# Expert layer of a perceiver block: token rows laid out in DRAM by expert, one weight row per expert and partition, six pairs held, eight experts fixed, fourteen narrow

## The chip, the core and the metric

The kernel runs on one core of a Trainium2 chip. A core has a matrix engine (TensorE, PE in the profile; PEld is its weight load), a vector engine (VectorE, DVE), an activation engine (ScalarE, ACT), GpSimd (POOL) and SyncE (SP), and 16 DMA engines that move data between DRAM and on-chip memory. Plain transfers are started by SyncE and ScalarE; transfers whose rows are given by a list of indices (indirect transfers) are started by GpSimd. Each engine works through its own queue in order: an instruction that waits holds up everything behind it in that queue. The metric is the time of one execution on the device, in microseconds.

## The reference

One layer for 256 tokens of width 512: cross-attention to 4096 context tokens, a Mamba-2 mixer, and a mixture of 32 experts with 6 per token beside a shared expert, each with a layer norm ahead and a residual. What the change touches is the last part:

```python
x = x + xattn(layernorm(x), ctx, ...)            # 16 query heads, 4 key heads, 128 wide
x = x + mamba(layernorm(x), ...)                 # inner width 1024
h = layernorm(x)                                 # (256, 512)
scores = sigmoid(h @ gate_w)                     # (256, 32)
topk_w, topk_i = top_k(scores, 6)
topk_w = topk_w / (sum(topk_w) + 1e-20)
combine = sum(one_hot(topk_i, 32) * topk_w[..., None], axis=1)
g = einsum('td,edf->tef', h, wg)                 # wg, wu: (32, 512, 192)
u = einsum('td,edf->tef', h, wu)
routed = einsum('tef,efd,te->td', silu(g) * u, wd, combine)   # wd: (32, 192, 512)
shared = (silu(h @ sg) * (h @ su)) @ sd          # inner width 384
x = x + routed + shared
```

## The kernel before

Tokens are handled as two tiles of 128 (t = 0, 1). Attention takes about the first 750 us, the mixer runs until about 835 us, the experts fill the rest. All matmuls are in 32-bit floats.

**Order of the work.** The program text gives each instruction a priority. A planner replays the program with its own estimates of durations and puts, on each engine, the ready instruction that is earliest in the program first. The order per engine is then fixed; instructions further down in the text may stand earlier in a queue when they are ready earlier. While attention runs, seven large writes of zeros fill the DRAM buffer `xg` (`clear`, L519), so that unused rows are zero.

**Routing.** `route(t)` (L995) turns the normed rows, multiplies them with the gate, takes the best six and builds `hot` (one-hot, 6 x 32) and `mask` (their sum). `ranks(t)` (L1024) gives each token its rank within each expert, by a matmul with a triangular matrix. `places()` (L1033) needs the counts of both tiles. Experts 0 to 9 have fixed places. The other 22 are sorted by their number of tokens: the 10 busiest get places with 128 rows ("wide"), the last 12 get 64 rows each ("narrow"). A place is a position in the order of work. `rows()` (L1072) turns rank and place into a row number for each token and choice; `scatter(t)` (L1017) then writes the token's normed row to each of its six rows of `xg`, with one indirect transfer per choice. `weight_rows()` (L1087) works out from `places` which rows of the weights the gathers read, and writes them to `place`. Experts with more than 64 tokens in a narrow place (or more than 128 anywhere) set `crowded`, and a second, slower pass over all experts follows; the same list of rows sends their surplus tokens to a second region of `xg`, `MAIN` and beyond.

**Rounds.** Experts are worked in 16 pairs. In round n (L1490): gate and up of pair n (`gate_up`, L1394, whose matmuls have the line of the helper L216; narrow: `gate_up_halves`, matmuls L1353), fetch of the rows of pair n+2 (`fetch`, L1326), turning the rows of pair n+1 by TensorE (`turn`, transposes L1338), down of pair n-1 (`down`, L1430 and L1433; narrow: `down_halves`, L1375 and L1376), turning the hidden values of pair n (L1412, narrow L1366). `fetch` is a plain transfer on SyncE, as the rows of a place are at a fixed address. Four buffers hold fetched blocks: a wide pair takes two, a narrow one takes one. Pairs 0 and 1 (experts 0 to 3) are not fetched: TensorE picks their rows with one-hot matrices (`picks`, `ps_pick`, L1447). Results go to the buffer `ye`; the last three pairs are added up in PSUM instead. At the end, 12 indirect gathers (L1294) bring each token's rows back from `ye`, and L1302 adds them with their weights.

**Weights.** A pair has three pieces of 768 KB: gate and up of its first expert, gate and up of its second, and both down matrices. 15 pieces are held at a time (five pairs), in memory that attention and the mixer no longer need. Pieces of pairs 0 to 4 are loaded by SyncE (`load_weights`, L1149 to L1153) when their memory comes free. Later ones are gathered by GpSimd with `gather_weights` (L1158), five indirect transfers a pair: the two gate-up pieces as soon as the piece's previous user has done its gate and up, the down piece after its down.

The scatter and the fetch, as they are:

```python
G.indirect_dma_start(out=xg_rows[t * TOPK + k], in_=xn[:, t, :], in_offset=None,
                     out_offset=bass.IndirectOffsetOnAxis(ap=row[:, t, k:k + 1], axis=0))
...
nc.sync.dma_start(self.rows[n, i], xg[r:r + P, :])
```

Of the kernel before, what the change touches and what calls it, by code (L numbers as in the profile page):

```python
# [19 lines left out]
P = 128  # L20
# [34 lines left out]
NHELD = 5  # L55
FIXED = 2 * NHELD
# [3 lines left out]
TAIL = 6  # L60
ZROW = WIDE * P + (NE - WIDE - TAIL) * HALFP
MAIN = ZROW + TAIL * HALFP

# [8 lines left out]
def perceiver_layer(ctx: ExitStack, tc: tile.TileContext, a: dict, out: bass.AP):  # L72
# [50 lines left out]
    xg = tc.dram_tile((MAIN + NE * L, DM), FP, name="xg")  # L123
# [14 lines left out]
    def layer(ctx, bounded):  # L138
# [16 lines left out]
        place = keep.tile([P, NE - FIXED + (NE - FIXED) // 2], U32, name="place")  # L155
# [363 lines left out]
        def clear(n):  # L519

            blocks = (MAIN + NE * L) // P
            per = -(-blocks // (NC - 1))
            e0, e1 = n * per, min((n + 1) * per, blocks)
            zeros(xg[e0 * P:e1 * P, :].rearrange("(e p) d -> p e d", p=P),
                  xn[:, 0:1, :].to_broadcast([P, e1 - e0, DM]))
            if n == 0:
                for y, r0 in ((ye, ZROW), (ye2, NE * L)):
                    zeros(y[r0:, :], xn[:, 0, :])
# [452 lines left out]
        def routing_memory():  # L981
            r = carve(lacc[:, 1], (P,), (P,), (NE,), (NT, NE), (NT, NE), (NT, NE), (NT, NE), (NT, NE), (NT, 8), (NT, 8),
                      (NT, TOPK), (NT, TOPK), (NT,), (NT * TOPK, NE), (FT, L), (1,), (1,), (1,), (1,), (NE,), (NE,), (NE,), (NE,))
            names = ("iota", "before", "first", "gate", "ev", "mask", "rank", "dst", "m8", "idx", "rowf", "w8", "den", "hot", "act",
                     "p", "free", "key", "pos", "keys", "at", "less", "over")
# [47 lines left out]
        def places():  # L1033


            mask, first, pos, key, keys, at, less, over = (m[n] for n in ("mask", "first", "pos", "key", "keys", "at", "less", "over"))
# [31 lines left out]

            V.tensor_scalar(over, m["iota"][:, 0:NE], float(L), float(MAIN), ALU.mult, ALU.add)
            V.tensor_tensor(over, over, first, ALU.subtract)  # L1070

        def rows():  # L1072
# [4 lines left out]
            V.tensor_scalar(dst, dst, float(P), None, ALU.is_ge)  # L1077
            V.tensor_tensor(dst, dst, by_tile(m["over"]), ALU.mult)
            V.tensor_tensor(dst, dst, rank, ALU.add)
            V.tensor_tensor(dst, dst, by_tile(m["first"]), ALU.add)  # L1080
            for t in range(NT):
                hot = m["hot"][:, t]
                V.tensor_tensor(hot, hot, dst[:, t].unsqueeze(1).to_broadcast([P, TOPK, NE]), ALU.mult)
                V.tensor_reduce(m["rowf"][:, t, :], hot, AX.X, ALU.add)
                V.tensor_copy(row[:, t, :], m["rowf"][:, t, :])

        def weight_rows():  # L1087


            n = NE - FIXED  # L1090
            V.tensor_scalar(place_f[:, 0:n], expert, float(P), m["p"], ALU.mult, ALU.add)
            e2 = expert.rearrange("p (n i) -> p i n", i=2)
            for i in range(2):
                half = slice(i * HALFP, (i + 1) * HALFP)
                V.tensor_scalar(place_f[half, n:], e2[half, i], float(REST), m["p"][half], ALU.mult, ALU.add)
            V.tensor_scalar(place_f[HALFP:, n:], place_f[HALFP:, n:], -float(REST), None, ALU.add)
# [47 lines left out]
        slots, slots_of = [], {}  # L1144

        def load_weights(slot, n, j):

            if j < 2:
                nc.sync.dma_start(slot, a["gu"][2 * n + j])  # L1149
            else:  # L1150
                d = slot.rearrange("p (j n) -> p j n", j=3)
                nc.sync.dma_start(d[:, 0:2], a["down"][2 * n:2 * n + 2].rearrange("e p n -> p e n"))
                nc.sync.dma_start(d[:, 2], a["down_rest"][2 * n:2 * n + 2].rearrange("e p n -> (e p) n"))  # L1153

        def gather_weights(slot, n, j):

            def rows(out, src, c):
                G.indirect_dma_start(out=out, out_offset=None, in_=src.rearrange("e p n -> (e p) n"),  # L1158
                                     in_offset=bass.IndirectOffsetOnAxis(ap=place[:, c:c + 1], axis=0))
            s = 2 * n - FIXED  # L1160
            if j < 2:
                rows(slot, a["gu"], s + j)
            else:
                for i in range(2):
                    rows(slot[:, i * DM:(i + 1) * DM], a["down"], s + i)
                rows(slot[:, 2 * DM:], a["down_rest"], NE - FIXED + s // 2)

        def load_piece(p):
            if p < 3 * NP:
                slots_of[p] = slots[p % (3 * NHELD)]  # L1170
                (load_weights if p < 3 * NHELD else gather_weights)(slots_of[p], p // 3, p % 3)

        def load_into(*tiles):
            for tl in tiles:
                slots.append(carve(tl, (WGU,))[0])
                load_piece(len(slots) - 1)
# [25 lines left out]
        for fs in plan:  # L1202
# [19 lines left out]
        load_into(kv[NC][1])  # L1222
# [11 lines left out]
        load_into(*w_x, lacc[:, 0])  # L1234
# [13 lines left out]
        load_into(*w_z)  # L1248
        route(0)
        assemble(1)  # L1250
        turn_y(1)
        ranks(0)
        product, turn = shared_hidden(0)
        mamba_out(1)
        product()
        load_into(wvc, wkc, ctx0)
        load_into(*w_out)
        n = NE - FIXED
        pick, number, expert, place_f, member, member2, members = carve(
            m["kv", 1], (NT * HEAD, P), (P,), (n,), (n + n // 2,), (TAIL, NE), (TAIL, NE), (4 * TAIL,))  # L1260
# [3 lines left out]
        turn()  # L1264
        route(1)
        shared_down(0)
        product, turn = shared_hidden(1)
        product()
        ranks(1)
        places()  # L1270
        rows()
# [351 lines left out]
```

## Time and profile before

| | |
|---|---|
| median of 3 runs | 1005.68 us (1003.59 to 1006.84) |
| profiled execution | 1007.29 us, span 1005.60 us |
| TensorE busy | 975.4 us, 97% of the span |
| VectorE, ScalarE, GpSimd busy | 498.0, 387.3, 206.8 us |
| moved by the DMA engines | 133.24 MB, 133 GB/s over the span |
| indirect transfers on GpSimd's queue (q0) | 34.35 MB in 8,016 packets |
| stretch of the experts' rounds | from about 848 us to 998 us |

The page divides the span into 40 slices with a digit for the busy share of each engine, and lists groups of instructions by source line. More to the point here are views of a stretch of time: busy times in windows, the chain of work that ended last in order of time (each piece with its start, its length, its engine and its line), the waits of an engine's queue (who waited for whom, us in total, times, longest), and the transfers with their median time from issue to landing. "issue" is time in which an engine waited for nothing that the profile shows.

### The profile page before, as it was taken

The numbers are of one execution on the slowest core, as the hardware profiler recorded it, in microseconds if no ns is written. First come the engines' busy times: TensorE is split into PE (matmuls) and PEld (weight loads), VectorE is DVE, ScalarE is ACT, GpSimd is POOL, SyncE is SP. The second block draws the span as 40 slices with busy tenths as digits, with TensorE's granted clock in tenths as the row PEclk, the third lists the DMA queues.
The fourth block names the chain that finished last, engine by engine and source line by source line (L and its number), as shares of the span: only waits on it lengthen the run. The fifth ranks groups of instructions, "written<-read, shape, count | busy, mean of one in ns | idle before, by whom it ended". The sixth has DMA issues, their size and how long they took to land.

```text
span 1005.6 us, 8991 instructions
## 1 busy us (share of the span) xinstructions
PE 975.4 (97%) x2749; PEld 461.7 (46%) x2749; DVE 498.0 (50%) x992; ACT 387.3 (39%) x853; POOL 206.8 (21%) x214
## 2 busy tenths in 40 slices
PE   7999999999999999999999999999999998799996
PEld 3444444444444444444444444444556554455542
DVE  4455555455454454544544544566796557122124
ACT  3645544443443443443434434442363631122210
POOL 4443002001101100201200200000023313455533
PEclk9999999999999999999999999999999999799999
DMA  9735043123313314305305205410153545899954
GB/s 324 220 72 166 4 128 119 37 74 109 79 31 147 83 22 156 85 6 172 83 1 178 54 10 167 131 38 0 27 201 128 202 137 205 300 351 362 365 202 122
DMA packets 139467, 133.24 MB, mean 133 GB/s; under 512 B 80689, under 2 KB 100050, under 8 KB 138258
## 3 DMA queue, kind: packets, MB, share of 16 engines
q1 hardware_dynamic: 126928, 91.85, 29.3%
q0 software_dynamic: 8016, 34.35, 9.5%
q10 hardware_dynamic: 4466, 6.38, 1.8%
q8 instruction: 24, 0.39, 0.2%
q14 instruction: 33, 0.27, 0.1%
HBM read 89.28 MB, written 43.27 MB: 132 GB/s over the span
## 4 chain that ended last, share of the span: by engine, by line
PE 91%; DMA 3%; DVE 2%; POOL 1%; ACT 1%; issue 1%; SPq 0%; POOLq 0%; DVEq 0%; ACTq 0%
PE oT L590 23%; PE scT L565 23%; PE ps_kv L362 17%; PE ps_egu L216 4%; PE ps_self L216 3%; PE ps_v L216 2%; PE ps_o L786 2%; PE ps_ye L1430 2%; PE ps_k L216 1%; PE ps_xbc L216 1%; PE ps_out L976 1%; PE ps_egu L1353 1%; PE ps_sgu L216 1%; PE xgTp L1338 1%; PE total L1421 1%; DMA xg_sb<-xg 1%
## 5 line engine op out<-in xcount | busy, mean ns | idle before, releaser
L581 DVE TENSOR_TENSOR lacc<-lacc,prT 128x512 f32<-128x512 f32 x256 | 183.1, 716 | 240.3 <-ACT prT L571 239.5
L571 ACT ACTIVATE prT<-scT,bq,rk 128x512 f32<-128x512 f32 x256 | 198.8, 777 | 254.7 <-PE scT L565 242.1
L565 PE MATMUL scT<-qT,kT 128*128 128x512 f32 x536 | 270.9, 593 | 0.0
L590 PE MATMUL oT<-prT,v 128*128 128x512 f32 x528 | 268.1, 593 | 0.9 <-ACT prT L571 0.9
L590 PEld LDWEIGHTS oT<-prT,v 128*128 128x128 f32 x528 | 100.3, 190 | 127.0 <-issue 114.8
L565 PEld LDWEIGHTS scT<-qT,kT 128*128 128x128 f32 x536 | 101.5, 190 | 124.3 <-issue 121.7
L194 POOL TENSOR_TENSOR rk<-pv,mhalf 128x4 f32<-128x4 f32 x32 | 32.3, 1010 | 370.8 <-DVE pv L193 370.8
L362 PE MATMUL ps_kv<-wkv,fast 128*128 128x512 f32 x112 | 53.5, 592 | 0.0
L252 ACT ACTIVATE sq<-kraw 128x128 f32<-128x128 f32 x128 | 35.6, 278 | 45.2 <-DVE kraw L380 43.2
L362 PE MATMUL ps_kv<-wkv,ctx 128*128 128x512 f32 x112 | 52.8, 593 | 0.0
L362 PE MATMUL ps_kv<-fast,fast 128*128 128x512 f32 x112 | 52.6, 593 | 0.0
L596 DVE TENSOR_TENSOR oacc<-oT,oacc 128x512 f32<-128x512 f32 x64 | 43.7, 683 | 0.0
L1405 DVE TENSOR_TENSOR hid<-si,ps_egu 128x128 f32<-128x128 f32 x20 | 5.8, 288 | 62.6 <-ACT si L1403 62.6
L362 PEld LDWEIGHTS ps_kv<-wkv,ctx 128*128 128x128 f32 x112 | 21.3, 190 | 26.7 <-issue 23.6
L362 PEld LDWEIGHTS ps_kv<-wkv,fast 128*128 128x128 f32 x112 | 21.3, 190 | 26.7 <-issue 26.7
L362 PEld LDWEIGHTS ps_kv<-fast,fast 128*128 128x128 f32 x112 | 21.3, 190 | 26.7 <-issue 21.7
L356 POOL TENSOR_TENSOR fast<-ctx 128x512 f32<-128x512 f32 x7 | 9.5, 1363 | 113.1 <-PE ps_kv L362 94.2
L380 DVE TENSOR_TENSOR kraw<-ps_kv,fast 128x256 f32<-128x256 f32 x42 | 17.8, 425 | 28.0 <-PE ps_kv L362 28.0
L786 PE MATMUL ps_o<-wo,qT 128*128 128x512 f32 x64 | 28.8, 593 | 0.0
L216 PE MATMUL ps_self<-wq,xT 128*128 128x512 f32 x64 | 28.1, 593 | 0.0
L601 DVE RECIPROCAL lacc<-ps_l 128x512 f32<-128x512 f32 x8 | 26.8, 3348 | 0.1
L362 PE MATMUL ps_kv<-fast,ctx 128*128 128x512 f32 x56 | 26.3, 593 | 0.0
(379 smaller groups left out, 1127.6 us busy)
## 6 DMA issues: line engine op xcount, KB each, us to landing
xg<-xn SPq DMA_DIRECT2D x6, 3328.0 KB, 11.6
ctx<-in_ctxT_dram SPq DMA_DIRECT2D x7, 1024.0 KB, 5.2
kd<-tr SPq DMA_DIRECT2D x112, 64.0 KB, 2.2
kT<-kd SPq DMA_DIRECT2D x28, 256.0 KB, 2.8
ye<-y_sb ACTq DMA_DIRECT2D x23, 256.0 KB, 6.2
xg_sb<-xg SPq DMA_DIRECT2D x22, 256.0 KB, 7.6
wq<-in_wq_dram SPq DMA_DIRECT2D x4, 1024.0 KB, 14.2
wo<-in_wo_dram SPq DMA_DIRECT2D x4, 1024.0 KB, 8.0
```

The lines of the kernel that those rows point to most:

```text
L194: return G.tensor_tensor(dst, v[:, :n], mhalf[:, :n], ALU.pow)
L216: TE.matmul(ps, lhs(k), rhs_of(k), start=(k == 0), stop=(k == KD - 1))
L252: S.activation(sq[:, h, :], raw[:, h, :], AF.Square, accum_out=ss[:, h:h + 1])
L362: TE.matmul(ps, lhs(k), rhs(k), start=(start and k == 0), stop=(k == 1), skip_group_check=True)
L565: TE.matmul(sc, kT[:, g, i * P:(i + 1) * P], qT[:, t, heads4(g), :].rearrange("p h q -> p (h q)"), start=True, stop=True)
L571: S.activation(pr, sc, AF.Exp, bias=shift, scale=SCALE if r is None else r[:, i, g:g + 1])
L581: V.tensor_tensor(la, la, pr, ALU.add)
L590: TE.matmul(outs[g, t], v[:, i, g * HD:(g + 1) * HD], pr, start=(n == 0), stop=last)
L596: V.tensor_tensor(ov, outs.pop((g, t)), ov, ALU.add)
L601: V.reciprocal(rl, ps)
L786: TE.matmul(m["ps_o", t], aT[:, t, h, :], wo[j][:, h % 4, :], start=(h == 0), stop=(h == NH - 1))
L1430: TE.matmul(ps[i], h[:, i, :], wd[:, i, :], start=True, stop=False)
```

## The change

The rows of `xg` are laid out by expert: the row of a token is 256 times its expert plus its rank (`rows_of`), which needs no place. `rows_of(t)` and `scatter(t)` follow `ranks(t)` for each tile. The old row, now computed by `result_rows` after the picks, is used for the results in `ye` alone. The second region of `xg` goes, so it has 8,192 rows instead of 11,520, and the second pass reads the same rows.

`fetch` of a fixed pair remains a plain transfer on SyncE. That of a later pair becomes an indirect gather on GpSimd, with row numbers that `place_rows` works out from the places: one per block for a wide pair, two half blocks in one gather for a narrow pair.

Eight experts are fixed instead of ten. Then 10 wide places and 14 narrow ones follow (12 before). `experts` in DRAM holds gate, up and the first 128 rows of down of an expert as one row of 2,048 floats per partition. The remaining 64 rows of down of a pair are a piece of their own. A gathered pair takes three indirect transfers. Six pairs are held; four of them are loaded by SyncE, pairs 4 and 5 are gathered as soon as the places are known, and the pair n+5 is loaded after the down product of pair n-1, as a whole. `shared_down(0)` stands ahead of `route(1)`.

```diff
-NHELD = 5
-FIXED = 2 * NHELD
+WEX = WGU + DM
+NHELD = 6
+FIXED = 8
 WIDE = FIXED + 10
...
-    xg = tc.dram_tile((MAIN + NE * L, DM), FP, name="xg")
+    xg = tc.dram_tile((NE * L, DM), FP, name="xg")
...
+        def rows_of(t):
+            V.tensor_scalar(m["dst"][:, t], m["iota"][:, 0:NE], float(L), None, ALU.mult)
+            V.tensor_tensor(m["dst"][:, t], m["dst"][:, t], m["rank"][:, t], ALU.add)
+            V.tensor_tensor(own, m["hot"][:, t], m["dst"][:, t].unsqueeze(1).to_broadcast([P, TOPK, NE]), ALU.mult)
+            V.tensor_reduce(m["rowf"][:, t, :], own, AX.X, ALU.add)
+            V.tensor_copy(row[:, t, :], m["rowf"][:, t, :])
...
+        def place_rows():
+            n, w = NE - FIXED, WIDE - FIXED
+            p, half = m["p"], lambda i: slice(i * HALFP, (i + 1) * HALFP)
+            def pairs(to, experts, per):
+                e2 = experts.rearrange("p (n i) -> p i n", i=2)
+                for i in range(2):
+                    V.tensor_scalar(to[half(i)], e2[half(i), i], float(per), p[half(i)], ALU.mult, ALU.add)
+                V.tensor_scalar(to[half(1)], to[half(1)], -float(HALFP), None, ALU.add)
+            for to, experts, per in ((place_f[:, 0:n], expert, P), (place_f[:, n + n // 2:n + n // 2 + w], expert[:, 0:w], L)):
+                V.tensor_scalar(to, experts, float(per), p, ALU.mult, ALU.add)
+            pairs(place_f[:, n:n + n // 2], expert, REST)
+            pairs(place_f[:, n + n // 2 + w:], expert[:, w:], L)
             V.tensor_copy(place, place_f)
...
+        def rows_at(out, src, c):
+            G.indirect_dma_start(out=out, out_offset=None, in_=src,
+                                 in_offset=bass.IndirectOffsetOnAxis(ap=place[:, c:c + 1], axis=0))
+
+        def load_weights(to, n, fixed):
+            if fixed:
+                for i in range(2):
+                    nc.sync.dma_start(to[i], a["experts"][2 * n + i])
+                nc.sync.dma_start(to[2], a["down_rest"][2 * n:2 * n + 2].rearrange("e p n -> (e p) n"))
             else:
+                s = 2 * n - FIXED
                 for i in range(2):
+                    rows_at(to[i], a["experts"].rearrange("e p n -> (e p) n"), s + i)
+                rows_at(to[2], a["down_rest"].rearrange("e p n -> (e p) n"), NE - FIXED + s // 2)
+
+        def load_pair(n):
+            if n < NP:
+                k = n % NHELD
+                weights[n] = (held[2 * k], held[2 * k + 1], rests[k])
+                load_weights(weights[n], n, 2 * n < FIXED)
...
         ranks(0)
+        rows_of(0)
         product, turn = shared_hidden(0)
         mamba_out(1)
         product()
+        scatter(0)
...
         turn()
+        shared_down(0)
         route(1)
-        shared_down(0)
         product, turn = shared_hidden(1)
         product()
         ranks(1)
+        rows_of(1)
+        scatter(1)
         places()
-        rows()
-        for t in range(NT):
-            scatter(t)
+        place_rows()
...
         shares()
-        weight_rows()
         turn()
         shared_down(1)
+        hold(oacc.rearrange("p t g n -> p (t g n)")[:, 0:WEX], kv[NC][0])
+        for n in range(FIXED // 2, NHELD):
+            load_pair(n)
...
             def fetch(self, n, r0=None):
-                if r0 is None:
-                    r0 = [self.row0(n) + i * P for i in range(self.blocks(n))]
...
+                if r0 is None and 2 * n < FIXED:
+                    r0 = [(2 * n + i) * L for i in range(2)]
+                for i in range(self.blocks(n) if r0 is None else 2):
+                    to = self.rows[n, i] = self.e4.tile([P, DM], FP, tag="xg", name="xg_sb")
+                    if r0 is not None:
+                        nc.sync.dma_start(to, xg[r0[i]:r0[i] + P, :])
+                    else:
+                        first, s = NE - FIXED + (NE - FIXED) // 2, 2 * n - FIXED
+                        rows_at(to, xg, first + (s + i if 2 * n < WIDE else WIDE - FIXED + (2 * n - WIDE) // 2))
...
-                for j in range(2):
-                    load_piece(3 * (n + NHELD) + j)
...
                 if n > 0:
-                    load_piece(3 * (n - 1 + NHELD) + 2)
+                    load_pair(n - 1 + NHELD)
...
-    return {"gu": c(gu.reshape(NE, P, WGU)), "down": c(wd[:, 0:P]), "down_rest": c(wd[:, P:])}
+    return {"experts": c(np.concatenate([gu, wd[:, 0:P]], axis=2)), "down_rest": c(wd[:, P:])}
```

## The prediction

> **What bounds the kernel now.** I read the page first, then the windows of the last 160 us, the chain over 838 to 873, SyncE's waits and the timelines of VectorE, GpSimd and SyncE. TensorE is busy 97% of the span and is itself the chain through attention, so an edit there that leaves its matmuls alone is worth nothing. The windows (columns after the stretch: length, then busy time and instructions of PE, PEld, DVE, ACT and POOL, granted clock, DMA share, GB/s) show the one large hole:
>
> ```profile
> 848.20:862.50 14.30, 14.22 (x45) 7.26 (x43) 4.24 (x20) 2.43 (x7) 10.95 (x12) 1.00 0.57 208
> 862.50:872.70 10.20, 2.87 (x12) 2.50 (x13) 1.32 (x2) 1.12 (x2) 3.93 (x5) 0.61 0.98 364
> 872.70:910.00 37.30, 37.30 (x139) 20.86 (x138) 9.23 (x27) 7.78 (x18) 16.47 (x18) 0.97 0.96 342
> 910.00:945.00 35.00, 35.00 (x133) 19.52 (x133) 6.53 (x20) 8.74 (x20) 17.55 (x19) 1.00 0.99 364
> 945.00:972.00 27.00, 27.00 (x129) 10.62 (x127) 6.32 (x19) 6.63 (x16) 11.34 (x12) 1.00 0.79 294
> ```
>
> Pairs 0 and 1 run until 862.4, then TensorE stands still and its clock falls to 0.61. From 872.7 on it is full, although the transfer engines are 96 to 99% taken. What ends the hole is in the chain (start, length, what) and in SyncE's waits:
>
> ```profile
> 843.46 0.08 DVE row L1085
> ...
> 857.88 2.71 DMA xg<-xn,row
> ...
> 861.25 9.62 DMA xg_sb<-xg
> 870.91 1.12 PE xgTp L1338 x4
> 872.03 0.64 PE hidTp L1412 x3
> 872.67 6.37 PE ps_egu L216 x16
> 879.04 0.87 PE xgTp L1338 x8
> ```
> ```profile
> SPq L1331 <- DMA xg<-xn,row: 19.0, 1, 19.0
> ```
>
> The rows of all twelve scatters are ready only at 843.5, because they need every expert's place. GpSimd then issues twelve scatters, 843.83 to 858.84, one each 1.27 us (0.96 busy, 0.30 issue); the last lands at 860.6. Only then does SyncE fetch pair 2, and the second block lands at 870.87, beside weight gathers GpSimd has just started.
>
> **1. Scatter by expert: the hole goes.** A row is now expert x 256 + rank. Tile 0's six scatters need only its ranks (L1031, 816.74): five small VectorE operations, then 6 x 1.27 = 7.6 us of GpSimd, 818 to 826. Tile 1's ranks are ready at 834.66; its rows at about 835.8, its scatters end at 843.4 and land 2.7 us later (the median of that transfer), 846.1. SyncE has nothing left to wait for: its last fixed load waits for ctx0, free at 811.5. It fetches pairs 2 and 3 (four blocks, 1.05 MB, addresses fixed) at about 846 and shares the engines with the first gathers (pair 4, 2.36 MB): 3.4 MB at 364 GB/s is 9.4 us, landed by 856 even in the worst order. Pair 1's work covers TensorE until 861.29 + 1.13 = 862.42. Without the wait it then needs 0.87 (turn) + 0.48 + 5.16 (gate-up), ending at 868.93 instead of 879.04. **Gain 10.1 us**, the slow clock included (6.37 against 5.16). If the cover failed, each microsecond past 862.4 costs one.
>
> **2. One wide pair turns narrow.** By the chain a wide round is 0.87 + 1.72 + 1.06 + 0.48 + 5.16 = 9.29 us; two narrow gate-ups start at 954.90 and 960.50:
>
> ```profile
> 902.41 5.16 PE ps_egu L216 x16
> 907.58 0.87 PE xgTp L1338 x8
> 908.45 1.72 PE ps_ye L1430 x4
> 910.17 1.06 PE ps_ye L1433 x4
> 911.23 0.48 PE hidTp L1412 x3
> ...
> 954.90 2.73 PE ps_egu L1353 x16
> ...
> 960.50 2.73 PE ps_egu L1353 x16
> ```
>
> One wide fewer, one narrow more: **9.29 - 5.60 = 3.7 us gained**. The narrow experts still fit on these inputs: worked out from the reference's router, the 11th busiest free expert has 43 tokens, 64 fit; the branch for crowded experts is not taken.
>
> **3. VectorE before the first picks: a loss.** The picks start at 841.65, after the x_sb addition (L1139, 840.93), whose bank they need; its matmul was done at 839.57, so VectorE's order sets this. Tile 1's new row operations come before the places: by rows L1107 (0.17), L1108 (0.20), L1471 (0.34), L1473 (0.34), L1085 (0.15), less their overlap, 1.1 us on an engine that is full from 834.5 to 837.3. Behind it, place_rows has four small operations more (0.2 each, as L1095) and three of the old rows (L1076 to L1078, 0.65 together) plus L1070 leave: nothing net. The rest of the old rows and the clamped result rows move behind the picks, beside 7.1 us of pick matmuls, and are wanted only by the gathers at 975. **Take 1.0 us lost**; ends 0 (filling VectorE's 1.2 us idle before L1058) and 2. A gain of up to 2.1, all of TensorE's idle before the picks, stays possible through another order; it sets the low end.
>
> **4. GpSimd in the mixer.** Tile 0's scatters stand around the power at 821.24 (L194), which layernorm and then route(1) wait for. One scatter ahead of it costs at most 1.3 us, and route(1)'s mask is ready at 831.4 while TensorE runs the shared experts until 833.9: hidden. All six ahead: 825.6 - 821.2 = 4.4 us late, about 3.5 of it on TensorE. I take 0, since the power is earlier in the program and ready after two or three scatters; the other end goes into the range.
>
> **5. Weights.** A pair is now three gathers (two of 128 rows of 8 KB, one of 2 KB rows), not five: 3.8 instead of 6.3 us of GpSimd. In all 12 x 3 weight gathers + 17 block fetches = 53 issues against 55. A slot is now given back only after the down product, but with six pairs held a load has five rounds' time. From 843.6, in bytes: 12 pairs x 2.36 + 21 fetches x 0.26 + 22 result blocks x 0.26 = 39.6 MB; at 364 GB/s 109 us, done at 953. Pair 15 is wanted at 982.4 - 12.8 = 969.6, pair 13 at 953.3 with 2 x 2.36 MB (13 us) still behind it. Cost 0; a load late by more than these 13 to 16 us stops TensorE.
>
> **6. Fetches move to GpSimd's queue** from pair 4 on. The rows (issue engine, count, size, median us to landing):
>
> ```profile
> xg_sb<-xg SPq DMA_DIRECT2D x22, 256.0 KB, 7.6
> w_in<-in_down_rest_dram,place POOLq DMA_INDIRECT x5, 8.4
> ```
>
> On SyncE's queue a fetch takes 7.6 us, the last gather of a pair on GpSimd's 8.4: the move costs 0.8 us of latency. A fetch goes out when its buffer is turned (888.80, transposes at 888.17) and is wanted two rounds later (907.41), 18.6 us; narrow ones go four deep (951.78, wanted at 975.4). By the rows nothing. [...] I take 0 and keep 4 for the range. Waits of GpSimd on a buffer hold the loads behind it, but a buffer is turned 2.8 us before the slot of the next load is free.
>
> Smaller zero fill (11,520 to 8,192 rows, hidden behind attention's matmuls; TensorE would wait only if its key blocks came late, and it does not now), wp's memory and the early first load: 0.
>
> **Sum.** -10.1 - 3.7 + 1.0 = -12.8. The profiled execution took 1007.29 us, its span 1005.60: span 992.8, 994.5 in all. It was 1.6 over the median of the runs, so the forecast is 1005.68 - 12.8 = **992.9**. The tail after 972 moves with the rounds: TensorE is busy 25.23 of 25.70 us there, and GpSimd is free well before.
>
> **Rivals.** (a) *As summed*, 992.9, own range 989.5 to 995.5: 0.70. (b) *A new wait ahead of the experts*: six scatters before the power, 3.5 more, 996.4. For it: GpSimd is idle from 818 to 821, so a scatter enters at once; against: the order above. 0.11. (c) *Fetches behind weights*, 4 to 6 more, 997 to 999. For: DMA at 0.99; against: the 18 us lead. 0.12. (d) *The hole stays*: the gathers of pairs 4 and 5 (6 x 1.27) go ahead of tile 1's scatters, the last lands near 860 and pair 2 near 868; only the narrow pair is gained, 1003. Against: rows come before places on VectorE. 0.03. (e) *Slower: transfers pace the rounds*, in the narrow rounds on GpSimd's queue. 39.6 MB must pass; the run ends 3 us later than before when pair 15 lands 15.8 us past its time, at 985, a rate under 39.6 / 142 = 279 GB/s. Rows of 8 KB and gathered blocks are untried; 6 KB and 2 KB rows run at 342 to 364. At 275 the time is 1011. 0.04.
>
> 0.3% is 3 us, about what these runs can tell from no change (they spread over 3.3). Faster 0.70 + 0.11 + 0.12 = 0.93, same 0.03, slower 0.04. The range leaves out (d), (e) and a little of each side: 989.5 to 999.
>
> **What would show it.** Right: scatters in two groups, near 818 and 836; no idle TensorE at 862 and clock 1.00; pair 2's gate-up at 5.16; seven narrow gate-ups instead of six, those after the first 5.60 apart; picks at 842 to 843. Wrong: TensorE waiting on xg_sb or on weights after pair 3, the power (L194) late behind scatters, GB/s under 300 between 870 and 940.

## The result and the profile after

The changed kernel takes **998.55 us** (median of 6 runs, 997.40 to 1000.71) against 1005.73 us of the kernel before (6 runs, 1003.59 to 1006.84): ratio 0.9933, 95% interval 0.9917 to 0.9949, so 7.2 us less. In three later groups of runs the kernel before took 1007.56 to 1008.43 us (medians), and in one of them the changed kernel, run again, 997.79 us (ratio 0.9905, interval 0.989 to 0.992), 10.1 us less. Both kernels spread by 3 to 5 us from run to run. The forecast was 992.9, 12.8 less.

The profiled execution of the changed kernel took 998.33 us with a span of 996.6, 9.0 us below the span before. First the windows of the experts' rounds (columns as before: length, busy time and instructions of PE, PEld, DVE, ACT and POOL, granted clock, DMA share, GB/s):

```profile
846.00:861.25 15.25, 15.25 (x43) 7.62 (x42) 8.67 (x32) 2.31 (x5) 6.96 (x7) 0.94 0.90 350
861.25:866.60 5.35, 5.35 (x17) 2.39 (x15) 0.83 (x4) 0.66 (x2) 1.18 (x2) 1.00 0.46 184
866.60:874.00 7.40, 7.33 (x35) 4.86 (x34) 1.73 (x5) 2.31 (x5) 3.54 (x4) 1.00 0.98 338
874.00:910.00 36.00, 36.00 (x140) 19.92 (x138) 9.14 (x26) 8.52 (x19) 18.91 (x20) 1.00 0.95 343
910.00:945.00 35.00, 35.00 (x146) 17.21 (x145) 7.74 (x23) 8.41 (x19) 16.35 (x18) 1.00 0.99 381
```

TensorE has no hole left: 7.33 of 7.40 us where it had 2.87 of 10.20. The one blemish is the clock of 0.94 at the start. From 866.6 to 945 the transfer engines are as full as before (0.95 to 0.99), and TensorE does not wait for them. The fetch of pairs 2 and 3 goes out at 850.13 (SyncE's timeline, first line here), 3 us after GpSimd's last scatter ends (847.05), where it went out at 860.87 before. The chain of the changed kernel (start, length, what) runs through the place of the hole on TensorE alone:

```profile
850.13 2.18 SPq L1344 DMA_DIRECT2D xg_sb<-xg  x4
```
```profile
844.30 8.83 PE ps_pick L1466 x16
853.13 5.16 PE ps_egu L218 x16
...
866.77 1.02 PE xgTp L1354 x8
867.79 0.33 PE hidTp L1432 x3
...
868.18 5.40 PE ps_egu L218 x16
873.58 0.87 PE xgTp L1354 x8
...
940.14 2.73 PE ps_egu L1373 x16
...
945.74 2.73 PE ps_egu L1373 x16
```

From the start of gate_up(0) (852.97 in TensorE's timeline; 848.62 before) to the end of gate_up(2) it is 20.61 us where it was 30.42. The narrow gate-ups of pairs 10 and 11 start 5.60 apart. There are seven narrow gate-ups, the first at 933.68. But the picks took 8.83 us, where they took 7.13 before:

```profile
841.65 7.13 PE L1447 MATMUL ps_pick<-xc,xn 128*128 128x512 f32 x16 [2.08 <-DVE x_sb L1139]
```

**Where the 9.0 us of the two spans lie** (before against after, from the chains and TensorE's timelines): the store of the running sums in the mixer is issued 0.41 later (775.22 and 775.63), which is chance, as the runs below with the same attention have it at 774.54 to 776.88; from there to mamba_out(0) 1.02 more; from the first tile's ranks to the second's 1.43 more; from these to the picks 0.21 less; from the picks' start to gate_up(0) 1.70 more; gate_up(0) to the end of gate_up(2) 9.81 less; the further rounds up to the gate-up of pair 13 3.70 less (87.06 to 83.36); from there to the end of the span 0.16 more. Sum 9.00 less. So the experts' part gave what it was to give, and **the front gave back 4.4 us**. Most of the rest of this document is about those.

Three places of the front. First the power, the instruction of the second tile's layer norm that GpSimd does (`rs<-pv,mhalf`, L196). GpSimd's timeline (start, length, what, the idle time before it), then what waited for it on VectorE and on TensorE, and the same place of TensorE before:

```profile
820.07 1.10 POOL L1022 DMA_INDIRECT xg<-xn,row  x1 [5.56 <-DVE xc L1112]
821.48 0.98 POOL L1022 DMA_INDIRECT xg<-xn,row  x1 [0.30 <-issue]
822.76 0.96 POOL L1022 DMA_INDIRECT xg<-xn,row  x1 [0.30 <-issue]
824.03 0.96 POOL L1022 DMA_INDIRECT xg<-xn,row  x1 [0.30 <-issue]
825.01 0.59 POOL L196 TENSOR_TENSOR rs<-pv,mhalf 128x1 f32<-128x1 f32 x1
```
```profile
825.63 0.61 DVE L206 TENSOR_SCALAR xn<-x_sb,mv,rs 128x512 f32<-128x512 f32 x1 [3.04 <-issue]
```
```profile
826.76 0.55 PE L1141 MATMUL ps_sh<-ident,sh 128*128 128x128 f32 x3 [1.64 <-DVE sh L1136]
```
```profile
824.41 0.55 PE L1131 MATMUL ps_sh<-ident,sh 128*128 128x128 f32 x3 [0.28 <-DVE sh L1126]
```

The power's input `pv` is ready at 822.59 (0.15 us of VectorE at 822.44, in the chain), and four scatters stand ahead of it in the queue: it runs at 825.01, 2.4 us late. VectorE's next instruction, the normed row `xn`, comes only then, and the product `sh` of the shared expert stands behind `xn` on VectorE: TensorE's `ps_sgu`, which `sh` reads, ended at 825.12, and `sh` ran at 826.16. TensorE, which turns `sh`, idles 1.64 us where it idled 0.28. Second, the chain at the mixer, where a broadcast brings the running sums of the decays to all partitions (`lm<-sums`; it is a plain transfer, but GpSimd starts it), and its line in the transfers before (KB, us to landing):

```profile
777.52 9.31 DMA lm<-sums
...
786.90 1.28 ACT L850
788.19 0.63 ACT lm L850
```
```profile
lm<-sums POOLq DMA_DIRECT2D x1, 1024.0 KB, 8.2
```

The broadcast landed 9.31 us after its issue and ScalarE waited for it; before, it landed after 8.2 us, and ScalarE did not wait. Third, the windows around the picks:

```profile
842.50:844.30 1.80, 0.00 (x0) 0.00 (x1) 1.64 (x8) 0.00 (x0) 1.50 (x2) 1.00 0.67 259
844.30:846.00 1.70, 1.70 (x2) 0.79 (x3) 1.60 (x11) 0.00 (x0) 1.09 (x3) 0.52 0.43 164
846.00:848.00 2.00, 2.00 (x4) 0.86 (x3) 0.22 (x1) 0.00 (x0) 1.70 (x2) 0.55 0.54 211
848.00:850.00 2.00, 2.00 (x6) 0.80 (x6) 1.88 (x6) 0.22 (x1) 1.39 (x3) 1.00 0.58 125
```

TensorE idles for 1.86 us, and then the picks start at a low granted clock: over 844.30 to 848.00 it is 0.52 to 0.55, and in windows of 0.4 us it is 0.50 from 844.4 to 847.6, 0.75 in the next and 1.00 from 848.0 on, so half speed for about 3.4 us.

### The profile page after: what moved, and what is told of

It reads as the page before. It is cut to its first block, busy times and chain, and to the rows that moved or that the text cites. A ratio compares the mean times of both kernels' runs of the same rounds, so it can differ in the third digit from the quotient of the medians.

```text
span 996.6 us, 8898 instructions
## 1 busy us (share of the span) xinstructions
PE 970.6 (97%) x2742; PEld 456.7 (46%) x2742; DVE 499.3 (50%) x999; ACT 386.2 (39%) x851; POOL 204.8 (21%) x212
## 4 chain that ended last, share of the span: by engine, by line
PE 94%; DMA 2%; DVE 1%; ACT 1%; issue 1%; POOL 1%; SPq 0%; ACTq 0%; DVEq 0%
PE oT L592 23%; PE scT L567 23%; PE ps_kv L364 17%; PE ps_egu L218 5%; PE ps_self L218 3%; PE ps_v L218 2%; PE ps_o L788 2%; PE ps_egu L1373 2%; PE total L1441 2%; PE ps_ye L1450 2%; PE ps_k L218 1%; PE ps_out L978 1%; PE ps_xbc L218 1%; PE xgTp L1354 1%; PE ps_ye L1453 1%; DMA lm<-sums 1%
## 5 line engine op out<-in xcount | busy, mean ns | idle before, releaser
L196 POOL TENSOR_TENSOR rk<-pv,mhalf 128x4 f32<-128x4 f32 x32 | 32.3, 1009 | 371.1 <-DVE pv L195 371.1
```

The costliest lines, as they stand in the source:

```text
L196: return G.tensor_tensor(dst, v[:, :n], mhalf[:, :n], ALU.pow)
```

## The experiments

All were run in three groups, each with the kernel before beside it; the ratios are to that. The groups ran on three different chips, so a difference of medians counts first within a group. The last three columns are stretches of each kernel's profiled execution, read as differences of starts in its timelines: from the issue of the store of the running sums (L844, L842 before; it comes ahead of the broadcast) to the first product of mamba_out(0); from the first tile's rank products to the second's; and the length of the picks.

| kernel | median us | ratio, 95% interval | store to mamba_out(0) | ranks to ranks | picks |
|---|---|---|---|---|---|
| before | 1005.7 to 1008.4 | 1 | 17.40 | 17.53 | 7.13 |
| changed, first runs | 998.55 | 0.9933 [0.9917, 0.9949] | 18.42 | 18.96 | 8.83 |
| group 1: e1, power first | 997.46 | 0.9895 [0.988, 0.991] | 18.98 | 18.05 | 8.83 |
| e2, decays first | 997.38 | 0.9904 [0.9889, 0.9918] | 17.40 | 18.97 | 7.13 |
| e3, one wide pair back | 1001.83 | 0.9934 [0.992, 0.9947] | 18.37 | 20.66 | 8.59 |
| e4, scatters late again | 1005.98 | 0.999 [0.9981, 0.9999] | 18.29 | 18.04 | 7.13 |
| group 2: e0, changed again | 997.79 | 0.9905 [0.989, 0.992] | 17.39 | 18.98 | 7.13 |
| e6, power and decays first | 994.88 | 0.9869 [0.9852, 0.9886] | 17.40 | 18.04 | 8.70 |
| e8, four idle products | 997.58 | 0.9899 [0.9885, 0.9914] | 18.38 | 18.96 | 7.14 |
| e11, also gate and shared_down(1) first | 995.77 | 0.9879 [0.9863, 0.9896] | 17.40 | 17.52 | 8.80 |
| group 3: e5, five pairs held | 999.98 | 0.9914 [0.9898, 0.9929] | 18.99 | 18.97 | 8.76 |
| e10, power, decays, gate first | 996.25 | 0.9887 [0.9867, 0.9906] | 17.40 | 17.53 | 8.83 |
| e13, two idle products | 996.75 | 0.9883 [0.9866, 0.9901] | 18.88 | 18.96 | 7.10 |
| e12, e10 with two idle products | 994.25 | 0.9865 [0.9845, 0.9884] | 17.40 | 17.53 | 7.10 |

### What gives the gain: scatters, and the narrow pair

e4 puts both tiles' rows and scatters back behind the places, as before; layout, fetches and loads stay those of the change.

```diff
-        rows_of(0)
-        scatter(0)
-        rows_of(1)
-        scatter(1)
         places()
-        place_rows()
+        placed = place_rows()
+        with tc.issue_after(placed.ins):
+            for t in range(NT):
+                rows_of(t)
+        for t in range(NT):
+            scatter(t)
```

> The changed kernel with the row numbers computed after the places and all twelve scatters after that, the old order; layout, fetch by place, held pairs and narrow places stay. Theory (the early scatters are what closes the hole after pair 1): the last scatter lands near 863, pair 2 at 868 to 873, TensorE idles 3 to 7 us after pair 1 and its clock falls; the power of layernorm(1) is no longer held up (1.4 us back) and the row operations stand before the picks no more. Net 3 to 8 us slower than the changed kernel, span 1000 to 1004. Rival (fetching by place or six held pairs close the hole by themselves): no idle over 1 us after pair 1, span 995 to 997.

Measured 1005.98, almost all of the gain gone (by the spans of the profiled executions 5.5 us of it, 1002.1 against 996.6). From the start of gate_up(0) to the end of gate_up(2) e4 takes 29.61 us (849.06 to 878.67), against 20.61 and, before, 30.42. Its chain has the hole again, by the same two steps as before the change, scatters one by one and then the fetch:

```profile
854.36 2.55 DMA xg<-xn,row
856.91 5.29 DMA xg<-xn,row x2
...
863.56 6.52 DMA xg_sb<-xg
...
871.88 6.79 PE ps_egu L218 x16
```

So step 1 stands: the early scatter, not the new layout or the new gathers as such, closes the hole. The new weight rows and the fetch on GpSimd's queue have no run that takes them back alone; that they cost nothing is read from the trace, where TensorE does not wait for either.

e3 makes one pair wide again (twelve wide places behind the eight fixed, as many narrow ones as before):

```diff
-WIDE = FIXED + 10
+WIDE = FIXED + 12
```

> The changed kernel with twelve wide free places instead of ten, so six narrow pairs and one wide pair more, as before the change. Theory (a wide round costs 3.7 us of TensorE more than a narrow one): 3.7 us slower than the changed kernel, span 1000.3, ratio to before about 0.997. Rival (transfers pace the rounds, so the narrow pair brings little): under 1.5 us slower.

Measured 1001.83, 4.4 us over e1 and e2 and 4.0 over the changed kernel of the second group. In the profiles the stretch from the start of gate_up(2) to the end of the span is 131.87 us (869.73 to 1001.6) against 128.42 (868.18 to 996.6): 3.45 for the pair. Up to the start of the last addition on VectorE (994.40 and 988.90) it is 3.95; what comes from there to the end of the span takes 7.2 to 9.1 us in these profiles, whatever the edit. Step 2's 3.7 lies between.

### Two losses in the front

e1 lets the first scatters wait for the normed rows of mamba_out(1), so that the power goes first (`mamba_out` returns the last instruction of its layer norm):

```diff
-        mamba_out(1)
+        normed = mamba_out(1)
         product()
-        scatter(0)
+        with tc.issue_after(normed.ins):
+            scatter(0)
```

> The changed kernel with tile 0's six scatters queued on GpSimd behind the power of layernorm(1); nothing else differs. Theory (the four scatters ahead of the power cost TensorE 1.4 us before the ranks): the power starts within 0.2 us of its input (822.6) instead of 2.4 us later, ranks(1) and all behind it 1.4 us earlier, span 995.2 against 996.6, ratio to before about 0.992. Rival 1 (the holes at 825 to 828 are also what brings the clock down at the picks): the picks run at clock 1.00, 7.0 instead of 8.8 us, and the span falls by 3.3 us to 993.3. Rival 2 (TensorE's own work covers the power, as the forecast had it): no difference, 996.6.

GpSimd's and TensorE's timelines of e1:

```profile
823.07 0.55 POOL L196 TENSOR_TENSOR rs<-pv,mhalf 128x1 f32<-128x1 f32 x1 [8.16 <-DVE pv L195]
823.80 1.11 POOL L1022 DMA_INDIRECT xg<-xn,row  x1 [0.18 <-issue]
```
```profile
826.23 0.55 PE L1141 MATMUL ps_sh<-ident,sh 128*128 128x128 f32 x3 [0.72 <-DVE sh L1136]
```

The idle time of TensorE ahead of the turn of `sh` falls from 1.64 to 0.72 us, and from ranks to ranks it is 18.05 instead of 18.96: 0.91 of the 1.43 us comes back, where 1.4 were expected. Every kernel with this edit shows it (18.04 in e6), every one without shows 18.96 to 18.98 save e4, where no scatter is there to be in the way (18.04), and e3, of which below. The time of 997.46 is too near to the changed kernel's to show 0.9 us. The picks of 8.83 us are still there, so the hole behind the late power is not needed for them.

The other half microsecond of that stretch is the order of shared_down(0) and route(1), which the change had turned round and which my prediction did not cost. e10 turns it back (`route(1)` ahead of `shared_down(0)`), beside e1's and e2's edits:

> Power ahead of the scatters, decays' broadcast ahead of pair 0's loads, and the second tile's gate ahead of shared_down(0). From the first ranks to the second 17.5 us (19.0 in the changed kernel), and 17.4 us from the issue of the sums' store to mamba_out(0)'s first product. In time: 994.9 of the kernel with the first two alone, less 0.5 for the gate, 994.4. If the gate's half microsecond is given back ahead of the picks: 994.9.

The stretch falls to 17.53, the value before the change, to the hundredth, and the idle time ahead of `sh` to 0.28. So 0.92 + 0.51 account for it whole. In the median, 996.25, nothing of the half microsecond shows beside the 994.88 of e6 in another group; the intervals overlap.

e2 makes the first loads of weights (pair 0's two of 1 MB and the one behind them) wait for the broadcast, by a small copy out of `lm` into each load's target:

```diff
+        for tl in (*w_x, lacc[:, 0]):
+            G.tensor_copy(carve(tl, (WEX,))[0][:, 0:1], m["lm"][:, SH - 1, 0:1])
         hold(*w_x, lacc[:, 0])
```

> The changed kernel with the loads of pair 0 and of lacc's expert held until the broadcast of the decay sums (lm) has landed, by three one-column copies on GpSimd that read lm and write the loads' targets. Theory (the 1 MB loads share the engines with that broadcast and land it 1.0 us later): the broadcast lands within 5 us of its issue instead of 9.3, the product of mamba_out(0) starts 1.0 us earlier relative to the gates' matmuls, or more if the broadcast is then no longer last; span 995 to 995.6. Rival (something else in the mixer, as ScalarE's table loads, ends last there): under 0.3 us of difference although the broadcast lands early.

VectorE's first use of the decays in e2, and SyncE's loads, which now stand behind it:

```profile
781.72 3.64 DVE L849 TENSOR_SCALAR lm<-lm,xc 128x128 f32<-128x128 f32 x16
```
```profile
782.88 0.82 SPq L1165 DMA_DIRECT2D w_in<-in_experts_dram  x2
```

In the changed kernel pair 0's two loads went out at 777.32 and 780.89, the broadcast at 777.52, and that use came at 786.85; from 779 to 787 the transfer engines were taken for 0.92 to 1.01 and moved 377 to 426 GB/s. Store to mamba_out(0) is 17.40 us in every kernel with this edit (e2, e6, e10, e11, e12), and 18.29 to 18.99 in every other variant save e0, which drew 17.39. So the loss is 0.9 to 1.0 us in four kernels, 1.5 to 1.6 in three and nothing in e0, and it is from the loads. With the loads held the broadcast itself lands 5.2 us after its issue (e11) where it took 9.31. ScalarE's own chain lets 1 us of that through: ScalarE comes to L850 in e2 10.24 us after the store's issue and does not wait, in the changed kernel at 11.27, after 1.05 of waiting for the broadcast. The time is 997.38, too near to the changed kernel's to show 1 us.

e6 has both edits at once.

> Power ahead of the first scatters and the decays' broadcast ahead of pair 0's loads, both at once. If the two losses are separate pieces of one chain, they add: 0.92 + 1.0 = 1.9 us under the changed kernel, 996.6 us beside 998.5; mamba_out(0)'s ps_out 15.5 us after the broadcast's issue, and 18.0 us from the first ranks to the second. The rival, that one floor (ScalarE's or VectorE's chain) stands under both, lets only one of them come through: 997.5.

994.88 (993.66 to 997.97), 2.9 us below e0 of the same group where 1.9 were expected; ratios 0.9869 and 0.9905, intervals apart by a hair. Both stretches show their shortening, so the two losses add. e11 puts the second tile's gate, and shared_down(1) with its addition, first as well.

> Power ahead of the scatters, decays' broadcast ahead of the loads, the second tile's gate ahead of shared_down(0), and shared_down(1) with its addition ahead of the placing, so that the addition releases the picks' bank earlier. If all four are separate pieces: 0.92 + 1.0 + 0.5 + 0.6 = 3.0 us under the changed kernel, 995.5 us, and some 994.5 if the shorter idle ahead of the picks keeps the clock up. If the gate's and the addition's moves only shift VectorE's work, 996.6. If shared_down(1) ahead of the placing makes the places late for the fetches of pair 4 and the weights: over 998.

995.77: no better than e6. The picks' stretch did not shorten: from the second ranks to the first pick 7.72 us against 7.70 in the changed kernel. The addition (L1149) comes early, at 838.05, but the picks now stand behind the placing's products on TensorE, and start 0.46 us after VectorE's copy of them (L1061). This guess fell: the wait for the addition was the last one, and another stood right behind it.

### The picks at half clock

The changed kernel run again:

> The changed kernel once more, so that the other three runs of this group are set against it under the same conditions. The theory (the loss ahead of the picks is made of separate pieces: the scatters ahead of the power, the late broadcast of the decays, and picks at half clock in some executions): 998.5 us within 1, the picks either 7.1 us at a granted clock of 1.00 or 8.8 us at about 0.53. The rival for the picks (the half clock is a fixed property of this order of work): always 8.8 us at about 0.53.

TensorE's timeline of this execution:

```profile
844.60 7.13 PE L1466 MATMUL ps_pick<-xc,xn 128*128 128x512 f32 x16 [1.92 <-DVE x_sb L1149]
```

The same kernel, nearly the same idle time ahead (1.92 and 1.86 us), and full clock (1.00 in the windows from 844.6 to 852). So the 1.7 us come in some executions and not in others. Over the nine profiles of kernels with early scatters and nothing put into that idle time, seven show picks of 8.59 to 8.83 us, two picks of 7.13 (e0, e2). In e3 the clock also fell in another place, behind the idle time ahead of `sh` (0.65 and 0.67 in the windows from 827 to 832, where the changed kernel has 1.00), so that its stretch from ranks to ranks is 20.66, 1.69 over the others. In e5 the first products of mamba_out(0) were slow too: four of them took 3.17 us where e1 has 1.98, and the next product of `ps_sgu` starts 20.24 us after the first of them, where it is 18.54 in the others.

Why the clock falls in one execution and not in another no run shows; what it costs is in the windows. Of the nine of 0.4 us from 844.4 to 848.0 eight have 0.50 and one 0.75: by an estimate from these, 8 x 0.20 + 0.10 = 1.7 us of work lost, and 1.70 is what 8.83 is over 7.13. In e3 the clock was 0.50 over 845 to 848 and in e5 0.83 over 845 to 855 (1.00 in e0); for e1, e6, e10 and e11 the length of the picks alone stands for it. The idle time ahead of the picks is 1.86 to 1.92 us in these profiles (e11 aside, where small products interrupt it).

The length of the idle time alone does not decide: 1.92 us were followed by full clock in e0, 1.86 by half in the changed kernel, and behind 1.78 in e4 the picks took 7.13 us. Seven of all the profiles have 1.64 to 1.86 us of it ahead of mamba_out(0) and seven have 1.63 to 1.65 us ahead of `sh`; what followed was slow behind two of these fourteen (e5 and e3), but at seven of the nine picks. What else counts there, as the small products ahead of the picks or the gathers that run meanwhile, no run separates.

e8 and e13 fill the idle time ahead of the picks with products that nobody reads. They add work and change nothing else:

```diff
         shared_down(1)
+        for _ in range(2):
+            TE.matmul(bank("ps_sgu"), xn[:, 1, 0:P], pick[:, 1].rearrange("p e r -> p (e r)"),
+                      start=True, stop=True)
```

(e8: four of them, of `xn` with `xn`.)

> The changed kernel with four more products of 128x512 into a bank that nobody reads, put into TensorE's idle time just ahead of the picks. The theory that the half clock at the picks comes from this idle time: granted clock 1.00 there in every execution, picks 7.1 us, and the time 0 to 1.7 us lower than the changed kernel's, 997.7 us as the middle. The rival, that the half clock comes from something other than idle time (the load of the transfers, or the stretch of holes some 15 us earlier): the picks still take 8.8 us at about 0.53, and the time stays at 998.5. If the four products delay the picks instead, the stretch from shared_down(1) to the first pick grows by up to 1.9 us.

> The changed kernel with two idle products (4 records of 0.44 us, 1.8 us in all) just behind shared_down(1), so that they fit into the 1.9 us of idle time ahead of the picks instead of standing before them. If this idle time is what lets the clock fall: picks 7.1 us at 1.00 in the profile, no delay, 0 to 1.7 us under the changed kernel by how often its picks are slow, 996.9 as the middle, and a narrower spread of the single times. If the clock falls for another reason: picks of 8.7 us as often as before, 997.8.

TensorE's timeline of e13:

```profile
842.20 1.88 PE L1290 MATMUL ps_sgu<-xc,xn 128*128 128x512 f32 x4
844.37 7.10 PE L1468 MATMUL ps_pick<-xc,xn 128*128 128x512 f32 x16 [0.29 <-DVE x_sb L1149]
```

Picks of 7.10 to 7.14 us in both, and in e12 below (1.00 in the windows of e12 and e13): three of three at full clock, against two of nine. The single times say little: e8 spans 0.70 us (5 runs) and e13 0.64 (4 runs), where e0 spans 3.06 (6 runs), but e12 spans 2.13 (4 runs), and e1, which has no idle products, 1.17 (4 runs). In e8 the products delay the first pick by 0.8 us (8.50 from the second ranks, against 7.70), which eats the gain: 997.58. In e13 the delay is 0.15, and the median is 996.75, 1.0 under e0, in another group; the intervals overlap, so in the time the gain is not shown. If the nine profiles are taken as draws of one chance, 2 of 9, three that keep the clock by luck have a chance of (2/9)^3 = 1.1%. So filling the idle time keeps the clock up at the picks, as far as three profiles can show. Why the kernel before and e4, with 2.08 and 1.78 us of idle time at the same place, had picks of 7.13 us in their one profile each stays open; by the same odds, both by luck is 5%.

### Six pairs held

```diff
-NHELD = 6
+NHELD = 5
```

> The changed kernel with five pairs of weights held, as before, instead of six; nothing else. My step put the sixth pair at nothing: with narrow rounds of 5.6 us and 2.2 MB a pair, the loads of a pair take about as long as its round, and the wait for weights is nowhere in the trace. Theory: same time as the changed kernel, 997.8 us within 1. The rival, that the sixth pair is what keeps TensorE fed once the rounds are short: waits on weights in some of the narrow rounds, 1 to 5 us more, 999 to 1003.

999.98, 2.2 us over the changed kernel of the second group, though by ratio to the kernel before the two intervals overlap (0.9914 and 0.9905). In the profiles, from gate_up(2) to the end of the span it is 130.68 us against 128.42, 2.26 more; up to the start of the last addition on VectorE 1.64 more, and the rest lies behind it. The chain of e5 and TensorE's timeline say where the 1.6 begins.

```profile
953.96 0.95 POOL v L1158
954.91 0.30 issue
955.22 10.65 DMA xg_sb<-xg,place
```
```profile
965.91 1.31 PE L1354 MATMUL xgTp<-ident,xg_sb 128*128 128x128 f32 x8 [0.97 <-DMA xg_sb<-xg,place]
```

With five held, the last pair's loads go out late, the last two fetches stand behind them in GpSimd's queue (issued at 955.22 and 956.47; in the changed kernel at 948.47 and 949.72), and one lands 10.65 us on, 0.97 us after TensorE wants it. Later in the tail TensorE idles 1.18 us, waiting for VectorE, where the changed kernel has 0.78. This is like my rival (c), in the one place where the slack is gone; whether the fetch was slow because it stood behind the loads or because the engines were full (taken for 1.02 from 930 to 960) is not separated. Why the loads are late is in the windows: from 855 to 865 and from 865 to 875 the transfer engines of e5 are taken for 0.44 and 0.67, those of the changed kernel for 0.89 and 0.83; from 930 to 960 it is the other way round, 1.02 against 0.95. The sixth pair is loaded in an early lull. I had expected nothing, and it is worth 1.6 us by the profile.

### All that paid

e12 is e10 (power, decays and gate first) with e13's two idle products.

> Everything that paid, together: power first, decays first, gate first, and the two idle products ahead of the picks. If the pieces add: 994.4 less 0.5 to 1 for the clock, 993.6 us. If the idle products do nothing for the clock: 994.4.

994.25 us (994.08 to 996.21), ratio 0.9865 with an interval of 0.9845 to 0.9884: below both the kernel before and the changed one (0.989 to 0.992). Beside e10 of the same group, which lacks only the idle products, it is 2.0 us less, but the intervals overlap. Its chain:

```profile
833.53 0.14 PE ps_rank L1031 x2
...
840.43 0.61 DVE x_sb L1149
841.17 7.10 PE ps_pick L1471 x16
848.27 5.16 PE ps_egu L218 x16
```

gate_up(0) starts at 848.27 where the changed kernel has 853.13 and its repetition 851.74. e6, without the idle products, lies within its spread.

## Why the prediction was right, and where it was not

The direction, the mechanism and the two large terms were right; the forecast was 5.65 us too low against the first runs. The time lies in the range of 989.5 to 999 by 0.45 us and above the 995.5 up to which I let the sum alone reach. The upper part was there for rivals (b) and (c), and of these only 0.92 us of (b) came; the rest of the overshoot came from terms that I had at nothing or not at all. So that it stayed inside is in part luck. Of the signs of being wrong that I had named one was seen, the late power; the picks came at 844.30, not at 842 to 843. Both groups of scatters came 2 to 3.5 us later than forecast (from 820.07 and 839.50), and the fetch at 850.13 instead of 846, which pair 1's work, to 866.77, still covered.

Of the 5.65, 1.8 is a step outside the kernel: I subtracted 1.6 because the profiled execution of before lay that much over the median of three runs, but it was the runs of that first group that were low (median 1005.73 of six): the medians of 25, 11 and 9 later runs are 1007.6, 1007.9 and 1008.4. The changed kernel's profiled run lies 0.2 under its own median. Against its own time, 1007.29, the sum said 994.5 and 998.33 came out, 3.8 over. By steps:

- **Step 1, the hole, -10.1**: measured -9.81. The slow clock after the hole (0.61 from 862.50 to 872.70) counted in it, and it went too (1.00 from 861.25 to 874). e4 shows it from the other side.
- **Step 2, one pair narrow, -3.7**: measured -3.70, and 3.45 to 3.95 in e3.
- **Step 3, VectorE ahead of the picks, +1.0**: failed, -0.21. The new row operations went into a wait of VectorE for TensorE, the low end that I had named; I took the middle. The wait ahead of VectorE's first copy of the places was 1.21 us and is 0.64 now, and e4, with the row operations behind the places, needs 7.63 us from the second ranks to the picks where the changed kernel needs 7.70:

```profile
838.56 0.19 DVE L1058 COPY lacc<-ps_place 128x32 f32<-128x32 f32 x1 [1.21 <-PE ps_place L1057]
```
```profile
841.42 0.19 DVE L1060 COPY lacc<-ps_place 128x32 f32<-128x32 f32 x1 [0.64 <-PE ps_place L1059]
```

- **Step 4, the power behind the scatters, 0**: failed, and I had both ends in hand. "Ready after two or three scatters" held: the power was ready at 822.59, before the third scatter began at 822.76. But the order in the queue is fixed beforehand by the planner's estimates, and it had put four scatters ahead, so the power was 2.4 us late. I had checked the way through route(1)'s mask and found it hidden; the delay took another, through `xn` and `sh` on VectorE to TensorE's turn of `sh`, and 0.92 us of it reached the second ranks. Rival (b) was this delay with all six ahead, and 3.5.
- **Step 5, weights, 0**: no wait for weights in the changed kernel, as I said. But "the early first load: 0", behind step 6, failed: 1.0 us, since loads of 1 MB run beside a broadcast on the chain, which took 9.31 us with them and 5.2 with the loads held (e11). I looked at what a load is late for, and not at what it makes late. The worth of the sixth pair, 1.6 us in e5, I had not named; the 0 took it as given.
- **Step 6, fetches on GpSimd's queue, 0**: right, with the sixth pair. The 4 us that I had kept in the range, and the 4 to 6 of rival (c), were an estimate of mine that no trace showed. With six pairs held no fetch was waited for, and with five one was, by 0.97 us; that its place behind the loads did it no run shows.
- **Not in the sum**: shared_down(0) ahead of route(1), 0.51, an edit that the diff shows and I passed over; and the picks' clock, 1.70, in seven of nine profiles. I had the idle time in view ("all of TensorE's idle before the picks") but not the clock after it.

The differences from the sum, in the profiled executions, add up: 1.43 (power, and the order of shared_down(0) and route(1)) + 1.02 (loads) + 1.70 (picks' clock) + 0.41 (chance in attention) + 0.16 (end) - 1.21 (step 3) + 0.29 (step 1) = 3.8.

## What to carry to other kernels

When work moves to an earlier place, ask of each queue that it enters what becomes ready just after it, and which transfer on the chain it runs beside: here four scatters of 1.27 us ahead of the power cost 0.92 us, and loads of 1 MB beside the broadcast 1.02, though no engine waited for the scatters or the loads themselves. Where the order of a queue is fixed by estimates, look in the trace at what stands ahead of an instruction on the chain, and follow its result to the engine behind it. Here 1.86 to 1.92 us of idle TensorE ahead of the picks were followed by picks 1.5 to 1.7 us longer in seven of nine profiles (at a clock of 0.50 in the changed kernel's) and not in the other two; two products that nobody reads are a cheap test, and in the two profiles that had them (e13, e12) the clock was 1.00. One profile of each kernel can't tell such a draw from an effect of the change: run the same kernel twice.

## What the runs showed of the hardware

In the changed kernel the granted clock was 0.50 for about 3.4 us after only 1.86 us of idle TensorE. In seven of nine profiles, with 1.86 to 1.90 us of it (in e11 broken up by small products), the picks took 8.59 to 8.83 us instead of 7.13. Behind two of fourteen idle stretches of 1.63 to 1.86 us elsewhere the work was slow too, in e3 at a clock of 0.65 to 0.67. The broadcast of 1 MB to 128 partitions was used by VectorE 5 us after its issue where SyncE issued no load before 782.88 (e2: 776.77 and 781.72), and landed in 9.31 us in the changed kernel, with 1 MB loads issued at 777.32, 780.89 and 782.81. The transfer engines moved 421 GB/s in 850 to 853 of the changed kernel and 406 over 930 to 960 of e5, more than the 364 that I had reckoned with. In e2, ScalarE stood still for 3 us right after the picks, and TensorE waited 0.36 us for what came behind,

```profile
851.64 3.02 another core or an unknown queue
```

while the transfer engines were full (taken for 1.03 from 850 to 856, 384 GB/s); no run here says what ScalarE waited for.
